# Attention with image prompts on one core: last keys in array halves, context 1 turned by VectorE, prompts in four tiles, inner products moved up, and loads on GpSimd's queue

## The chip, the core and the metric

The kernel runs on one core of a Trainium2 chip. The core has five engines that run side by side, each through its own instructions in order: TensorE (PE in the profile; PEld is its loading of weights, which overlaps with its products), VectorE (DVE), ScalarE (ACT), GpSimd (POOL) and SyncE (SP). They work on SBUF, a memory of 128 partitions, and on PSUM, into which TensorE writes; PSUM has eight banks of 512 float32 per partition. Engines wait for each other by semaphores. Transfers between main memory and SBUF are issued by SP, ACT or POOL and carried out by 16 DMA engines. All data here are float32.

The metric is the time of one execution in microseconds of device time, as the median over several runs. The profile comes from one further execution.

## What is computed

Eight batches (B = 8). Each has 112 queries of 320 channels and a context of 375 rows of 512, of which the last four are image prompts (NIP = 4) and the other 371 are text. There are 20 heads of 16 channels.

```python
q, k_t, v_t = heads(x @ W_q), heads(text @ W_k), heads(text @ W_v)
probs_t = softmax(q @ k_t.T * 16 ** -0.5)             # 112 x 371 for each head
text_out = probs_t @ v_t
k_ip, v_ip = heads(ip @ W_k_ip), heads(ip @ W_v_ip)
qsem = l2norm(probs_t @ text)                         # 112 x 512 for each head
sem = qsem @ l2norm(ip).T                             # 112 x 4
probs_ip = softmax(q @ k_ip.T * 16 ** -0.5 + 0.5 * sem) * spatial_mask
out = (text_out + probs_ip @ v_ip) @ W_out + b_out + x
```

The kernel never forms `probs_t @ text`. Its squared norm is p G p, where p are the unnormalised probabilities and G = text textᵀ, the inner products of the context's rows with each other; G is the same for all heads of a batch. G is symmetric, so only its upper part is made, its diagonal blocks are halved and all of it is doubled.

## The kernel before

**Layout.** Channels lie in three chunks on the partitions: two of 128 and a last one of 64 (`FULL` = 2, `REST` = 64). Heads are worked in five groups of four (`g` = 0 to 4). A head's scores use one of the four 32-row strips of the array (`RG` = 32), so the four heads of a group go side by side. Groups 0 to 3 use the two full chunks; a strip of 32 rows holds two heads there, and a mask on the queries (`emask`, line 353) picks one. Group 4 uses the last chunk. Its 64 channels hold four heads in two strips, so the kernel before spreads them: `spread` (L124) puts 16 columns of zeros behind each head's columns in the last chunk of `W_q` and `W_k`, which makes it 128 wide.

**Keys.** `keys(b)` (L493) makes kT, the channels' chunks by 371 context rows, in three pieces. The first two are full-array products of `wk_sb` with the transposed context `ctxT` (L512). The third is made in two ways. For batches 0 and 7 it is a product like the others with the spread weights (L512 for batch 0, `last_keys`, L526, for batch 7). For batches 1 to 6 `values(b)` (L535) carries 64 extra columns of key weights beside the 320 of `W_v` (L543, 384 wide), POOL spreads the result into `k3` (L552), and three PE transposes (L503) turn it.

**Context.** A context reaches `ctxT` (512 by 384, in four chunks of 128) in one of two ways. For b below `LEAD` = 2, rows are loaded as they are (L156, L158), turned by 12 PE transposes (L414) and copied out of PSUM by ACT and DVE (L422, L424). From batch 2 on, eight transfers (L143, L148) load 32-row blocks of 128 columns and DVE turns them in three stream transposes (L402).

**A group's work.** Scores (L662) on PE; negative row maximum on DVE (L675); exponentials on ACT (L679); a transfer on SP that deals the probabilities into 32-row blocks (`xg`, L686); a stream transpose on DVE (L698, `transposed`); then the big products on PE, probabilities times `u` (L710, `product`), which holds, for each context row, its part of G, a column of ones, the prompts' columns and the values of the group. `placed` (L629) is the POOL copy that puts the next group's values into `u`; it can only run when PE has read the old ones. The product is reduced against p on DVE (L763) and its last 21 columns are copied by ACT (L737). Scores run two groups ahead.

**Next batch's work.** Between groups the function `behind(n)` puts pieces for the next batch on PE: inner products (`gram`, L474, in four column tiles of 32), values, keys, queries (`project_queries`, L319). Its list `turn` says from which pool each piece takes its PSUM bank: `mm` and `sc` have two banks, `qd` has four, which also hold the big products. G goes to `u` through SP (`gram_to_groups`, L488), values through main memory (L561, L573, L582).

**Order.** Every engine's order is the order in which the code is written. The first stage (L1020 to L1064) is written out piece by piece: context 0, its inner products, values and queries of batch 0, first keys, first scores, then context 1's transposes, the second scores, the other keys, and the first of three pieces of batch 1's inner products. `alone(0)` then runs the first group of big products, `behind(0)` puts in the other two pieces of inner products, the prompts' projections (`prompt_projections`, L275; their weights are loaded into `wip` by L1057 and L1058) and one values chunk, and pairs of groups follow. The last batch has its own order from L1314.

**Prompts.** `normalised_prompts` (L247) makes the transposed prompts for all batches at once (32 of them). Their keys and values are two column tiles of 32 rows (L280). `prompt_values` (L589) loads a batch's prompt values, repeated over the 112 partitions, by a transfer on SP; `x_sb`, the queries' input and the residual, is loaded by SP in three parts (L167, L1196, L1236).

Of the kernel before, what the change touches and what calls it, by code (L numbers as in the profile page):

```python
# [20 lines left out]
def kernel(  # L21
# [30 lines left out]
    HN = H * NIP  # L52
    VW = NIP + 1 + D
# [51 lines left out]
    wk_sb = const.tile([P, NE, CP], F32, tag="wk_sb", name="wk_sb")  # L105

    wv_sb = const.tile([P, NE, C + REST], F32, tag="wv_sb", name="wv_sb")
# [16 lines left out]
    def spread(eng, t):  # L124

        v = t[:, :, FULL * P :].rearrange("p k (a r d) -> p k a r d", r=2, d=D)
        for a in (3, 2, 1):
            eng.tensor_copy(v[:, :, a, 0, :], v[:, :, a // 2, a % 2, :])
        eng.memset(v[:, :, :, 1, :], 0.0)


# [3 lines left out]
    def load_ctx(b):  # L135
        ct = io.tile([P, NT, E], F32, tag="ct", name=f"ct_{b}")
        if b >= LEAD:
# [78 lines left out]
    k3 = const.tile([P, NT, GROUP, 2, D], F32, tag="k3", name="k3")  # L216

    def more_constants():
        halves(1)
        nc.gpsimd.memset(k3[:, :, :, 1, :], 0.0)  # L220
        nc.gpsimd.memset(wo_sb[REST:, FULL, :], 0.0)
        for at in attn_ring:
            nc.gpsimd.memset(at[:, C:], 0.0)
# [10 lines left out]
    def order_values():  # L234
# [10 lines left out]
        )  # L245

# [28 lines left out]
    def prompt_projections():  # L275

        ps = bank("ps_kv")
        for e in range(NE):
            for i, w in enumerate((wkip_sb, wvip_sb)):
                nc.tensor.matmul(  # L280
                    ps[i * N : (i + 1) * N, :C],
                    ipT[:, e, :],
                    w[:, e, :],
                    start=(e == 0),
                    stop=(e == NE - 1),
                )
        kv = work.tile([2 * N, C], F32, tag="vip", name="kv", bufs=1)
        nc.scalar.copy(kv, ps[: 2 * N, :C])
        k3p = k3[:N, 0]
        nc.gpsimd.tensor_copy(  # L290
            k3p[:, :, 0, :], kv[:N, FULL * P :].rearrange("n (a d) -> n a d", d=D)
        )
# [3 lines left out]
        for i in range(NC):  # L296
            nc.tensor.transpose(
                ps[:, i * N : (i + 1) * N],
                kv[:N, i * P : (i + 1) * P] if i < FULL else k3p.rearrange("n a r d -> n (a r d)"),
                ident[:N, :N],  # L300
# [11 lines left out]
        nc.sync.dma_start(vipd, kv[N:])  # L312
# [6 lines left out]
    def project_queries(bs):  # L319
# [21 lines left out]
        for i in range(NC):  # L341
# [10 lines left out]
            for r in range(2 if i < FULL else 1):  # L352
# [14 lines left out]
    def begin(b):  # L367
        s = st[b] = dict(ct=loaded.pop(b))
        s["ctxT"] = work.tile([P, NE, TP], F32, tag="ctxT", name=f"ctxT_{b}")
        if b < LEAD:  # L370
            nc.gpsimd.memset(s["ctxT"][:, :, T:], 0.0)

        s["kT"] = work.tile([P, NC, T], F32, tag="kT", name=f"kT_{b}")
        s["k3"] = k3
# [19 lines left out]
    def transposed_context(b):  # L394
# [3 lines left out]
        if b >= LEAD:  # L398
# [94 lines left out]
    def keys(b):  # L493
# [3 lines left out]
        for i in range(NC):  # L497
            ps = bank(f"ps_k_{b}_{i}", spare=0 < b < B - 1 and i == FULL)
            if 0 < b < B - 1 and i == FULL:

                for c in range(NT):
                    rows = min(P, TT - c * P)
                    nc.tensor.transpose(  # L503
                        ps[:, c * P : c * P + rows],
                        s["k3"][:rows, c].rearrange("p a r d -> p (a r d)"),
                        ident[:rows, :rows],
                    )
                nc.scalar.copy(s["kT"][:, i, :TT], ps[:, :TT])
                yield
                return  # L510
# [9 lines left out]
            yield  # L520

    def last_keys(b, ps):

        s = st[b]
        for e in range(NE):
            nc.tensor.matmul(  # L526
                ps[:, :TT],
                wk_sb[:, e, FULL * P :],
                s["ctxT"][:, e, :TT],
                start=(e == 0),  # L530
                stop=(e == NE - 1),
            )
        nc.scalar.copy(s["kT"][:, FULL, :TT], ps[:, :TT])

    def values(b):  # L535
        s = st[b]
        s["vext"] = work.tile([P, NT, C + REST], F32, tag="vext", name=f"vext_{b}", bufs=1)
        ctxT, vext = s["ctxT"], s["vext"]
        w = C + REST if 0 < b < B - 1 else C
        for c in range(NT):  # L540
            ps = bank(f"ps_v_{b}_{c}")
            for e in range(NE):
                nc.tensor.matmul(  # L543
                    ps[:, :w],
                    ctxT[:, e, c * P : (c + 1) * P],
                    wv_sb[:, e, :w],
# [887 lines left out]
```

## Time and profile before

| | |
|---|---|
| median of 3 runs | 419.94 us (419.73 to 420.93) |
| the profiled execution | 421.54 us |
| its span, first to last instruction | 419.8 us |
| granted TensorE clock | 0.999 |
| busy PE, PEld, DVE, ACT, POOL | 411.7, 314.1, 322.2, 185.5, 116.0 us |
| main memory read, written | 19.04 MB, 5.22 MB |

The page of the profile lists busy time by engine, a picture of the span in 40 slices, DMA queues, the chain of work that ended last, and the costliest groups of instructions. The chain is followed back from the last instruction: at each step to what released it, or to the instruction before it on its engine. A group's row reads: line, engine, operation, output from input with partitions by elements, count, then busy time and the mean length of one in ns, then the idle time just before them and what ended it. Instructions on PE overlap, so the mean length of one is longer than the busy time that it adds. A timeline row starts with start and length; a row of stretches has a stretch, its length, and busy times of PE, PEld, DVE, ACT and POOL, the granted clock, the DMA engines' busy share and GB/s. Rows whose engine is written SPq or POOL with `DMA_DIRECT2D` are the issuing of transfers, not the transfers.

### The profile page before, as it was taken

The numbers are of one execution on the slowest core, as the hardware profiler recorded it, in microseconds if no ns is written. First come the engines' busy times: TensorE is split into PE (matmuls) and PEld (weight loads), VectorE is DVE, ScalarE is ACT, GpSimd is POOL, SyncE is SP. The second block draws the span as 40 slices with busy tenths as digits, with TensorE's granted clock in tenths as the row PEclk, the third lists the DMA queues.
The fourth block names the chain that finished last, engine by engine and source line by source line (L and its number), as shares of the span: only waits on it lengthen the run. The fifth ranks groups of instructions, "written<-read, shape, count | busy, mean of one in ns | idle before, by whom it ended". The sixth has DMA issues, their size and how long they took to land.

```text
span 419.8 us, 13826 instructions
## 1 busy us (share of the span) xinstructions
PE 411.7 (98%) x5511; PEld 314.1 (75%) x5511; DVE 322.2 (77%) x684; ACT 185.5 (44%) x634; POOL 116.0 (28%) x278
## 2 busy tenths in 40 slices
PE   8999999999999999999999999999999999999995
PEld 8866686877677786868686877778776888776893
DVE  4054777897887876886888897887788897789964
ACT  3253333334543642514553464333643464246772
POOL 4302310031161352012051225102124126005570
PEclk9999999999999999999999999999999999999999
DMA  8678966778554656577645575575656345575311
GB/s 249 163 190 246 220 157 165 180 187 181 133 156 125 169 127 170 143 162 160 174 116 138 148 173 144 156 186 138 164 150 168 92 118 149 156 177 169 98 34 29
DMA packets 58002, 64.64 MB, mean 154 GB/s; under 512 B 19016, under 2 KB 51760, under 8 KB 57938
## 3 DMA queue, kind: packets, MB, share of 16 engines
q1 hardware_dynamic: 57054, 62.32, 58.5%
q8 instruction: 44, 0.72, 0.7%
q10 hardware_dynamic: 692, 0.89, 0.7%
q0 software_dynamic: 192, 0.55, 0.6%
q14 instruction: 20, 0.16, 0.1%
HBM read 19.04 MB, written 5.22 MB: 58 GB/s over the span
## 4 chain that ended last, share of the span: by engine, by line
PE 87%; DVE 4%; DMA 3%; ACT 2%; SPq 2%; issue 1%; ACTq 0%; POOL 0%; DVEq 0%; POOLq 0%
PE ps_qd L710 39%; PE ps_v L543 15%; PE ps_k L512 10%; PE ps_g L474 8%; PE ps_s L662 5%; PE ps_q L344 3%; PE ps_o L867 2%; DMA xg<-p 1%; DVE xgT L698 1%; PE ps_g L444 1%; DMA vr<-vd 1%; ACT p L679 1%; PE ps_c L414 1%; DVE nmx L675 1%; SPq L488 1%; DMA ct<-in_ctx_dram 1%
## 5 line engine op out<-in xcount | busy, mean ns | idle before, releaser
L710 PE MATMUL ps_qd<-u,xgT 32*112 32x40 f32 (+11 forms) x3840 | 215.7, 351 | 0.4 <-DVE xgT L698 0.4
L710 PEld LDWEIGHTS ps_qd<-u,xgT 32*112 32x112 f32 x3840 | 177.4, 172 | 38.4 <-issue 7.1
L698 DVE STREAM_TRANSPOSE xgT<-xg 128x768 f32<-128x768 f32 (+1 forms) x63 | 123.1, 1976 | 7.1 <-DMA xg<-p 7.1
L679 ACT ACTIVATE p<-ps_s,nmx 112x371 f32<-112x371 f32 x160 | 85.6, 584 | 58.3 <-DVE nmx L675 57.2
L675 DVE TENSOR_REDUCE nmx<-ps_s 112x1 f32<-112x371 f32 x160 | 77.1, 534 | 36.7 <-PE ps_s L662 34.0
L763 DVE CUSTOM_DVE_ANT_0 p<-ps_qd,p 112x371 f32<-112x371 f32 x150 | 72.7, 544 | 15.9 <-ACT pvs L737 10.4
L629 POOL COPY u<-vr 128x64 f32<-128x64 f32 x120 | 26.7, 236 | 185.0 <-PE ps_qd L710 108.0
L543 PE MATMUL ps_v<-wv_sb,ctxT 128*128 128x384 f32 (+1 forms) x192 | 63.8, 479 | 0.3 <-ACT kT L519 0.3
L662 PE MATMUL ps_s<-kT,qm 32*112 32x375 f32 (+1 forms) x320 | 60.8, 486 | 0.0
L543 PEld LDWEIGHTS ps_v<-wv_sb,ctxT 128*128 128x128 f32 x192 | 35.3, 190 | 21.2 <-ACT kT L519 1.2
L512 PE MATMUL ps_k<-ctxT,wk_sb 128*128 128x371 f32 x136 | 45.8, 481 | 0.0
L737 ACT COPY pvs<-ps_qd 112x21 f32<-112x21 f32 x150 | 21.7, 198 | 52.4 <-DVE ss L763 50.1
L512 PEld LDWEIGHTS ps_k<-ctxT,wk_sb 128*128 128x128 f32 x136 | 24.6, 190 | 13.4 <-ACT ctxT L424 0.5
L474 PE MATMUL ps_g<-ctxT 128*32 128x119 f32 (+11 forms) x672 | 33.3, 344 | 0.6 <-POOL ctxT L390 0.6
L474 PEld LDWEIGHTS ps_g<-ctxT 128*32 128x32 f32 x672 | 25.9, 109 | 8.1 <-issue 4.1
L662 PEld LDWEIGHTS ps_s<-kT,qm 32*112 32x112 f32 x320 | 27.1, 171 | 5.0 <-issue 0.5
L550 ACT COPY vext<-ps_v 128x384 f32<-128x384 f32 (+1 forms) x24 | 11.2, 465 | 37.1 <-PE ps_v L543 37.0
L681 ACT COPY ipl<-ps_s 112x4 f32<-112x4 f32 x140 | 24.0, 172 | 0.0
L353 DVE TENSOR_SCALAR qm<-ps_q,emask 128x224 f32<-128x224 f32 (+1 forms) x25 | 9.0, 398 | 18.5 <-PE ps_q L344 18.5
L460 ACT ACTIVATE ug<-ps_g 128x375 f32<-128x375 f32 (+2 forms) x24 | 9.0, 377 | 29.2 <-DMA ct<-in_ctx_dram 8.4
L519 ACT COPY kT<-ps_k 128x371 f32<-128x371 f32 x17 | 8.0, 469 | 30.5 <-PE ps_k L512 30.5
L402 DVE STREAM_TRANSPOSE ctxT<-ct 128x512 f32<-128x512 f32 x18 | 19.3, 1077 | 0.0
(157 smaller groups left out, 311.6 us busy)
## 6 DMA issues: line engine op xcount, KB each, us to landing
xg<-p SPq DMA_DIRECT2D x158, 162.3 KB
u<-ug SPq DMA_DIRECT2D x128, 99.0 KB
ct<-in_ctx_dram SPq DMA_DIRECT2D x24, 176.0 KB
vip<-vipd SPq DMA_DIRECT2D x7, 560.0 KB
vr<-vd SPq DMA_DIRECT2D x20, 120.0 KB
vd<-vext SPq DMA_DIRECT2D x14, 160.0 KB
vd<-vext SPq DMA_DIRECT2D x28, 40.0 KB
ct<-in_ctx_dram SPq DMA_DIRECT2D x4, 256.0 KB
```

The costliest lines, as they stand in the source:

```text
L474: nc.tensor.matmul(ps[p * RG : (p + 1) * RG, s0 : T - t0], ctxT[:, e, t0 + q * RG : t0 + (q + 1) * RG], ctxT[:, e, t0 + s0 : T], start=(e ...
L512: nc.tensor.matmul(ps[:, :TT], wk_sb[:, e, i * P : (i + 1) * P], s["ctxT"][:, e, :TT], start=(e == 0), stop=(e == NE - 1),)
L543: nc.tensor.matmul(ps[:, :w], ctxT[:, e, c * P : (c + 1) * P], wv_sb[:, e, :w], start=(e == 0), stop=(e == NE - 1),)
L629: nc.gpsimd.tensor_copy(region(b, c)[:, :, UV - c * P :], s["vr"][:, c * QN : (c + 1) * QN, g, :])
L662: nc.tensor.matmul(ps[:S, :w], qm[a * RG : (a + 1) * RG, i, r, j * S : (j + 1) * S], s["kT"][a * RG : (a + 1) * RG, i, :w], start=True, st ...
L675: nc.vector.tensor_reduce(nmx, ps[:S, :TT], AX.X, ALU.max, negate=True)
L679: nc.scalar.activation(p, ps[:S, :TT], AF.Exp, bias=nmx)
L681: nc.scalar.copy(s["ipl"][:, groups[g][a], :], ps[:S, TT:T])
L698: nc.vector.transpose(xT[:, j : j + n].rearrange("p j (k q) -> p q j k", q=QN), xg[:, :, j * RG : (j + n) * RG].rearrange("p q (j k) -> p ...
L710: nc.tensor.matmul(banks[a][:S, j * RG : UW], xT[a * RG : (a + 1) * RG, j, :S], region(b, c)[a * RG : (a + 1) * RG, p, q * RG :], start=(j ...
L737: nc.scalar.copy(s["pvs"][:, h, :], ps[:S, TT:UW])
L763: nc.vector.tensor_tensor_reduce(out=p, in0=ps[:S, :TT], in1=p, scale=1.0, scalar=0.0, op0=ALU.mult, op1=ALU.add, accum_out=s["ss"][:, h : ...
```

## The change

1. **Last keys in array halves.** `last_keys` serves all batches. The 64 key columns are no longer spread. Each of the four chunks of E is multiplied twice, into the PSUM partitions 0 to 63 for the first half of the context's rows (`KH` = 186) and into 64 to 127 for the second half. ACT copies each half twice, so that kT's last chunk holds the 64 channels two times, on partitions 0 to 63 and 64 to 127. `W_q`'s last 64 columns are likewise there twice, by one POOL copy. Group 4 then works as the others do: `scores` takes strips 0, 2, 1, 3 for its four heads, with the mask; so queries need both masks in the last chunk too (`range(2)`, one more DVE operation for each projection). Gone are `spread`, `k3` with its copies and transposes, and the 64 extra columns of the values.
2. **Context 1 by VectorE.** Context 1 is loaded and turned as batches 2 to 7 are, and its place is earlier: right after batch 0's inner products in the code.
3. **Prompts in four tiles.** Keys and values of the prompts are four column tiles of 32 rows and 160 columns; three ACT copies and one POOL copy take them out, and two transfers instead of one write the values to main memory.
4. **Inner products moved up.** All three pieces of batch 1's inner products stand in the first stage, before the first big products; `behind(0)` has none.
5. **GpSimd's queue.** `prompt_values` and the second and third part of `x_sb` are issued by POOL instead of SP.

The lists of banks (`turn`) are changed accordingly.

```diff
-            if 0 < b < B - 1 and i == FULL:
-                for c in range(NT):
-                    rows = min(P, TT - c * P)
-                    nc.tensor.transpose(
-                        ps[:, c * P : c * P + rows],
-                        s["k3"][:rows, c].rearrange("p a r d -> p (a r d)"),
-                        ident[:rows, :rows],
-                    )
...
+        last_keys(b, bank(f"ps_k_{b}_{FULL}", spare=0 < b < B - 1))
+        yield
...
     def last_keys(b, ps):
         s = st[b]
         for e in range(NE):
...
+            for n in range(2):
+                nc.tensor.matmul(
+                    ps[n * REST : (n + 1) * REST, : min((n + 1) * KH, TT) - n * KH],
+                    wk_sb[:, e, FULL * P :],
+                    s["ctxT"][:, e, n * KH : min((n + 1) * KH, TT)],
+                    start=(e == 0),
+                    stop=(e == NE - 1),
+                )
+        for n in range(2):
+            t = slice(n * KH, min((n + 1) * KH, TT))
+            for m in range(2):
+                nc.scalar.copy(
+                    s["kT"][m * REST : (m + 1) * REST, FULL, t],
+                    ps[n * REST : (n + 1) * REST, : t.stop - t.start],
+                )
...
-        w = C + REST if 0 < b < B - 1 else C
...
-                    wv_sb[:, e, :w],
+                    wv_sb[:, e, :],
...
+        rg = a
+        if i == FULL:
+            rg, r = a // 2 + 2 * (a % 2), a % 2
...
-        if b >= LEAD:
+        if b > 0:
...
             for i, w in enumerate((wkip_sb, wvip_sb)):
...
+                for n, part in enumerate(parts):
+                    m = 2 * i + n
+                    nc.tensor.matmul(
+                        ps[m * N : (m + 1) * N, : C // 2],
+                        ipT[:, e, :],
+                        w[:, e, part],
...
-        nc.sync.dma_start(
+        nc.gpsimd.dma_start(
             st[b]["vip"].rearrange("p n h d -> p (n h d)"),
...
     drain(products)
+    drain(transposed_context(1))
     gram_to_groups(0, range(QN - 1))
...
-    spread(nc.gpsimd, wq_sb)
-    nc.gpsimd.tensor_copy(wv_sb[:, :, C:], wk_sb[:, :, FULL * P : C])
-    spread(nc.gpsimd, wk_sb)
+    nc.gpsimd.tensor_copy(wq_sb[:, :, C:], wq_sb[:, :, FULL * P : C])
...
-    turn[:] = ["mm", "qd", "qd"]
-    drain(transposed_context(1))
-    prompts_behind(1)
...
-    run(("g", 1), lambda: gram(1))
+    turn[:] = ["mm", "mm", "sc"]
+    run(("g", 1), lambda: gram(1), NT)
...
-                turn[:] = ["sc", "mm", "qd", "mm"]
-                nc.sync.dma_start(x_sb[:, 1:5, :], x[1:5].rearrange("b s c -> s b c"))
+                turn[:] = ["qd", "mm"]
+                nc.gpsimd.dma_start(x_sb[:, 1:5, :], x[1:5].rearrange("b s c -> s b c"))
...
-            gr(nb, 2)
             if n:
+                gr(nb, 2)
                 f(b - 1)
...
-                nc.sync.dma_start(x_sb[:, 5:, :], x[5:].rearrange("b s c -> s b c"))
+                nc.gpsimd.dma_start(x_sb[:, 5:, :], x[5:].rearrange("b s c -> s b c"))
```

83 lines of the change are left out of this document (27 added, 56 removed).

## The prediction

> **What bounds the kernel now.** I read the page from the top, then the chain, then the groups by shape.
>
> ```profile
> span 419.8 us, 13826 instructions
> ...
> PE 411.7 (98%) x5511; PEld 314.1 (75%) x5511; DVE 322.2 (77%) x684; ACT 185.5 (44%) x634; POOL 116.0 (28%) x278
> ...
> PE 87%; DVE 4%; DMA 3%; ACT 2%; SPq 2%; issue 1%; ACTq 0%; POOL 0%; DVEq 0%; POOLq 0%
> ```
>
> PE is busy for 98% of the span and carries 87% of the chain; the next engine, DVE, has 77%. So a microsecond of PE work removed is a microsecond of time, unless PE then waits for something. Two stretches say where DVE could take over (columns: stretch, length, then busy time of PE, PEld, DVE, ACT, POOL, each with its count):
>
> ```profile
> 109.00:158.00 49.00, 49.00 (x763) 37.23 (x762) 40.81 (x91) 23.41 (x86) 17.85 (x31) 1.00 0.55 141
> ...
> 378.00:392.00 14.00, 14.00 (x221) 10.32 (x220) 13.39 (x27) 9.68 (x33) 8.06 (x15) 1.00 0.52 149
> ```
>
> In mid-kernel DVE has 8.2 us free in 49, ACT half of it, POOL most of it. In the ending (378 to 392) DVE is nearly as full as PE, and a gain on PE alone is worth little there.
>
> The chain in order of time gives the price of each PE piece (start, length, piece, instructions):
>
> ```profile
> 13.69 2.16 PE ps_v L543 x8
> ...
> 25.22 0.85 PE ps_q L344 x6
> 26.07 1.43 PE ps_c L414 x12
> 27.50 1.21 PE ps_s L662 x6
> 28.70 5.18 PE ps_k L512 x16
> 33.89 2.64 PE ps_g L474 x27
> 36.53 1.15 PE ps_qd L710 x10
> ...
> 41.88 2.19 PE ps_g L474 x43
> 44.07 2.21 PE ps_kv L280 x16
> 46.28 2.78 PE ps_v L543 x8
> 49.05 1.15 PE ps_qd L710 x10
> ...
> 101.51 0.32 PE ps_k L503 x3
> 101.83 2.51 PE ps_k L512 x8
> 104.34 5.16 PE ps_v L543 x16
> ...
> 138.09 0.47 PE ps_k L503 x3
> 138.56 4.64 PE ps_g L474 x71
> 143.19 2.78 PE ps_v L543 x8
> ```
>
> Three prices follow. Each matrix product in the code is issued as two instructions (eight for four chunks of E). Batch 0's values, 320 columns wide, take 2.16/8/320 = 0.844 ns per column and instruction; the later ones, 384 wide, 2.58 (5.16/2), which is 0.42 more. Second, column tiles stream side by side: the prompts' 16 instructions of 320 columns in two tiles take 2.21, as long as 8 of them would (2.16). Third, a change of tile shape costs 0.15 to 0.20: the three key transposes take 0.47 between inner products and other shapes and 0.32 among full-array work, and the first values after another shape 2.78 against 2.58.
>
> **The change, part by part, in PE time.**
>
> *Keys' last 64 channels.* They come from two half-array tiles of 186 columns: 16 instructions, 8 side by side, 8 x 186 x 0.844 = 1.26. No row has 64-column tiles; the nearest are the 32-column tiles above, so 1.26 is the low end, and the high end is the two halves one after the other, 2.51. I take 1.26, because the prompts' row shows two tiles at the price of one. With a shape change in (0.15) and, where full-array work follows, one out (0.20):
> - batch 0: 2.59 (half of 5.18) becomes 1.41, -1.18.
> - batches 2, 4, 6 (inner products follow): the transposes' 0.47 become 1.41, +0.94; three value chunks lose 3 x 0.42 = 1.26. Net -0.32 each.
> - batches 1, 3, 5 (full-array work on both sides): 0.32 becomes 1.61, +1.29, against -1.26: nothing. Here the change only pays for itself.
> - batch 7: 2.59 becomes 1.41, -1.18 on PE, in the ending.
>
> The Trainium skill (TensorEngine Tiling (Array Packing), Key Properties) says that changing the tiling mode, not just the tile, drains TensorE. The trace agrees on the sign with the 0.15 and 0.20 above; were the drains free, batches 1, 3 and 5 would gain 0.32 each and the sum would be about 1 us better.
>
> *Context 1 by DVE.* PE loses 1.43 (12 transposes), DVE gets three stream transposes of 1.077 for one copy, ACT loses two copies:
>
> ```profile
> L402 DVE STREAM_TRANSPOSE ctxT<-ct 128x512 f32<-128x512 f32 x18 | 19.3, 1077 | 0.0
> L353 DVE TENSOR_SCALAR qm<-ps_q,emask 128x224 f32<-128x224 f32 x15 | 6.1, 444 | 4.0 <-PE ps_q L344 4.0
> ...
> L508 ACT COPY kT<-ps_k 128x371 f32<-128x371 f32 x6 | 3.0, 507 | 1.1 <-PE ps_k L503 1.1
> ...
> L339 ACT COPY xT<-ps_x 64x224 f32<-64x224 f32 x3 | 1.1, 352 | 0.0
> ```
>
> The transposes stand in DVE's hole of 11.40 us ahead of the first masked queries, so they cost nothing if the context has landed. The danger is the queue behind them. POOL's copy of batch 1's prompts waits for the last transpose, and behind it, on POOL, now stand the zeroing of xT and the copy of wq_sb, which ran from 14.56; PE needs the zeros by about 20.4:
>
> ```profile
> 14.56 0.28 POOL L327 MEMSET xT<- 64x224 f32 x1
> ...
> 20.30 0.82 PE L344 MATMUL ps_q<-xT,wq_sb 128*128 128x112 f32 x6
> ...
> 21.16 0.58 DVE L353 TENSOR_SCALAR qm<-ps_q,emask 128x112 f32<-128x112 f32 x2 [11.40 <-PE ps_q L344]
> ```
>
> When does the context land? Now the loads are over by about 13.2 (15 packets in 13.2 to 14.5). It comes in rows of 512 B instead of 2 KB: four transfers of 352 rows and four of 19. Where such rows fill the queue they take 3 x 16 x 1.211/1219 = 47.7 ns each:
>
> ```profile
> DMA packets 15, 0.02 MB, mean 13 GB/s; under 512 B 7, under 2 KB 7, under 8 KB 15
> ```
> ```profile
> q1 hardware_dynamic: 1219, 0.61, 121.1%
> ```
>
> Over 16 engines 1408 rows take 4.2, some 2 more than now, so about 15; the 76 odd rows add 0.2 if spread and 3.6 if they all go through one engine. So the last rows land between 15.2 and 19. Two transposes need only the big transfers and end at 17.2; the third ends between 18.3 and 20.1, and POOL's copy and zeros (0.28 each at most) between 18.8 and 20.7. Against 20.4 that is a wait of 0 to 0.3; I take 0.2, and up to 1 for the range, because transfers of this stage may also meet others.
>
> *Inner products moved up.* No PE work changes, but the order does. These rows (the packets are those of 42.0 to 42.7) set the order's cost:
>
> ```profile
> 32.74 3.12 DVE L698 STREAM_TRANSPOSE xgT<-xg 128x768 f32<-128x768 f32 x2 [2.51 <-DMA xg<-p]
> ...
> 37.03 0.50 SPq L122 DMA_DIRECT2D wip<-in_L_xattn_W_v_ip_dram  x1
> ```
> ```profile
> DMA packets 105, 0.15 MB, mean 210 GB/s; under 512 B 6, under 2 KB 105, under 8 KB 105
> ```
> ```profile
> 43.97 4.50 DVE L698 STREAM_TRANSPOSE xgT<-xg 128x1536 f32<-128x1536 f32 x2
> ```
> ```profile
> L698 DVE STREAM_TRANSPOSE xgT<-xg 128x1536 f32<-128x1536 f32 x17 | 51.5, 3027 | 0.0
> ```
>
> Chain of the first stage: queries end at 26.07, scores 1.21, keys 2.59 and 1.41, whole inner products 4.64 (row at 138.56): 35.92. The first transposed probabilities, which hang on the first scores and not on what changes here, are there at 35.86, so the first big products start at 35.9 instead of 36.53 and end at 41.3 instead of 41.88. The cover is thus used to the end: any lateness of the probabilities now shows at once. Next come the prompts. Their 16 instructions become 32 of 160 columns in four tiles, 8 x 160 x 0.844 = 1.08, -1.1. But their weights are asked for at 37.03 now, at the end of a run of issues on SP that starts from the first scores and does not change. The packets between 42.0 and 42.7 are all under 2 KB, so the weights' 5 KB packets have started by then, and I let them land by 42.7. The prompts' bank is now one of the four that the big products hold; DVE frees the first when the first of its four sums is done, and it begins them when the products end, so before 42.7 too.
>
> So PE stands idle from 41.3 to 42.7, does the prompts until 43.8 and a values chunk (2.78 - 0.42) until 46.2. DVE, whose group transposes started at 43.97 behind the sums of the first products, starts 0.6 earlier, and its first transposition (3.0) ends at 46.4. The second group starts at 46.4 instead of 49.05: **-2.65** of a PE saving of 1.43 + 1.18 + 1.1 + 0.42 = 4.13. The weights' late landing, hidden today under 2.19 of inner products, takes most of the rest.
>
> *After that:* batch 1's two other value chunks -0.84 and its keys +1.29: +0.45; batches 2, 4, 6: -0.96; 3 and 5: 0.06. Together **-0.45**. Ending: -1.18 on PE beside a full DVE, and the bank is held longer by four ACT copies; I take **-0.3**, ends 0 and -1.2.
>
> *Cover.* ACT's four copies of 64 x 186 stand for one of 507: by the 352 row at most 4 x 0.35 = 1.4, +0.9 per batch, some 7 in all, on an engine 56% idle; a bank comes free 0.9 later, under inner products of 4.64 or keys of 2.51. DVE gets a second masking of the last queries, four of 0.444 and a shorter one, within its 8.2 free per 49. The spreading and key copies on POOL go.
>
> *POOL's queue.* POOL issues two loads of x and seven prompt-value transfers in SP's place:
>
> ```profile
> L118 POOL DMA_DIRECT2D wo_sb<-in_L_xattn_W_out_dram x1 | 0.9, 921 | 0.0
> ...
> L1219 POOL DMA_DIRECT2D bias_sb<-in_L_xattn_b_out_dram x1 | 0.5, 543 | 0.0
> ...
> L629 POOL COPY u<-vr 128x64 f32<-128x64 f32 x120 | 26.7, 236 | 185.0 <-PE ps_qd L710 108.0 <-DMA u<-ug 30.0 <-DMA vr<-vd 24.0
> ```
>
> 112 rows cost 0.543, 256 cost 0.921, so 2.6 ns a row more: seven of 0.54, and about 1.4 and 1.1 for the 448 and 336 rows of x, 6.3 in all. Behind them stand the placements (L629) that PE needs; these waited 108 us for PE itself, so I take 0, with 6.3 as the far end. On SP nine issues go and four come (context 1 in eight transfers, not four); I count nothing for either.
>
> **Sum.** 0.2 - 2.65 - 0.45 - 0.3 = -3.2. The profiled execution took 421.54, with a span of 419.8; less 3.2 that is 418.3 and 416.6. The median of the runs is 419.94, 1.6 below the profiled one, which gives 416.7.
>
> **Rivals.**
> - *The gain passes whole* (weights and banks early enough, ending follows PE): 4.13 + 0.45 + 1.18 = -5.8, 414.2. For it: PE carries the chain. Against: the landing at 42.
> - *The halves do not run side by side.* Then batches 0 to 6 cost 1.25 more each, 8.75, and batch 7's 0.3 is lost: 425.7, slower than before. It decides from 3.2/56 = 57 ns per step: above 214 instead of 157. Against it: the prompts' row; for it: two tiles of 64 need double the weights per step.
> - *POOL becomes the queue PE waits for*, by its transfers or the zeros behind the context: up to 6.3, 423; it decides when half of that shows.
> - *Shape changes dearer* for 64-column tiles, 0.5 (the longest wait before big products that the profile puts down to issue, below) instead of 0.15 (eight times) and 0.20 (three times): +3.7, 420.4, no change.
>
> ```profile
> PEld ps_qd L710 <- issue: 7.1, 16, 0.5
> ```
>
> **How the numbers follow.** Measurement tells 0.3%, 1.3 us, from no change: faster below 418.7, slower above 421.2. Chances: forecast 0.62 (own range 415.2 to 418.6), whole gain 0.14, shape changes 0.08, halves 0.07, POOL 0.09. So faster 0.76, same 0.08, slower 0.16. The range from 414.0 to 421.0 leaves out the slower cases and a little below.
>
> **What would show it.** In the new profile: 16 key instructions at about 1.3 to 1.4 in the chain; values at 2.16; prompts at 1.1 after a PE gap of about 1.4 near 41 to 43; second group of big products near 46.4; PE before the first queries waiting 0.2 or less on POOL; 378 reached about 3.1 earlier. The forecast is wrong if the halves take 2.5, if L629 delays PE, or if the context lands after 20.

## The result, and the profile after

The changed kernel takes 433.52 us (median of four runs, 428.47 to 434.83), the kernel before 420.44 in the same session. The ratio is 1.0279, with a 95% interval of 1.0223 to 1.0334: slower by 2.8%, where 416.7 us and a gain of 0.8% were forecast. Some executions of a kernel are slower as a whole, at a lower granted clock; the ratios, here and below, leave these out, while the medians take them in.

The page of the profile after (the queue lines are packets, MB and share of 16 engines):

```profile
span 431.8 us, 14046 instructions
...
PE 418.2 (97%) x5609; PEld 329.4 (76%) x5609; DVE 325.4 (75%) x691; ACT 190.3 (44%) x658; POOL 117.2 (27%) x272
...
q1 hardware_dynamic: 56128, 57.29, 54.0%
q0 software_dynamic: 1328, 5.57, 5.2%
...
PE 87%; DMA 4%; DVE 3%; ACT 2%; issue 1%; SPq 1%; POOL 1%; ACTq 0%; DVEq 0%; POOLq 0%
```

PE's busy time has gone up by 6.5 us though the change takes work from it (e17 below, with the same 5609 instructions, is busy for 408.6); part of that is work at half clock, shown in the last section. POOL's queue (q0) now carries 5.57 MB. The chain in order of time (start, length, piece) shows where the time went:

```profile
37.98 6.61 DMA wip<-in_L_xattn_W_v_ip_dram
44.63 2.35 PE ps_kv L274 x28
46.98 2.86 PE ps_v L531 x8
49.84 1.15 PE ps_qd L695 x10
...
91.86 2.94 PE ps_qd L695 x66
94.80 0.70 issue
95.51 4.40 PE ps_qd L695 x48
...
103.78 1.41 PE ps_k L509 x15
...
107.87 4.31 PE ps_v L531 x16
...
151.09 2.93 PE ps_qd L695 x62
154.02 1.29 issue
155.31 6.08 PE ps_qd L695 x48
```

The prices of PE work are those forecast: last keys 1.41, values 4.31 for sixteen. What is new are waits. The prompts' product starts at 44.63, when its weights land; it then takes 2.35 instead of 1.1, at half clock (at the full clock, in e3 below, the same 28 of its 32 instructions take 1.28). And in the middle of the big products PE stops (the pieces named issue), first at 94.80, longest at 154.02. Around the second stop, with the half clock behind it, 4.9 us are lost: the lag behind the kernel before is 2.85 us at 148.82 and 7.75 where the next keys start. Of these 0.55 are not the stop's, since e1 below has no stop there and loses as much (e12 tells why).

The starts of the big products tell how much each stretch costs. The table gives, for some kernels of this study, the start of a group in us and in brackets its distance from the kernel before:

| kernel | batch 0, 2nd | batch 1, 1st | batch 1, 3rd | batch 2, 4th | batch 6, 4th | batch 7, 5th |
|---|---|---|---|---|---|---|
| before | 48.98 | 89.41 | 109.43 | 166.41 | 361.54 | 403.27 |
| after | 49.77 (+0.8) | 89.71 (+0.3) | 112.11 (+2.7) | 173.31 (+6.9) | 372.73 (+11.2) | 417.06 (+13.8) |
| e1, values on SP | 46.89 (-2.1) | 88.54 (-0.9) | 111.73 (+2.3) | 168.58 (+2.2) | 365.19 (+3.7) | 407.33 (+4.1) |
| e3, both on SP | 48.04 (-0.9) | 88.97 (-0.4) | 113.52 (+4.1) | 170.38 (+4.0) | 368.27 (+6.7) | 410.32 (+7.1) |
| e4, before, both on POOL | 48.54 (-0.4) | 88.97 (-0.4) | 108.99 (-0.4) | 168.29 (+1.9) | 366.23 (+4.7) | 409.60 (+6.3) |
| e9, e3 with loads put off | 47.80 (-1.2) | 87.74 (-1.7) | 108.18 (-1.3) | 166.40 (0.0) | 363.43 (+1.9) | 406.04 (+2.8) |
| e12, e3 with rows mended | 47.31 (-1.7) | 87.59 (-1.8) | 111.07 (+1.6) | 167.34 (+0.9) | 362.74 (+1.2) | 404.79 (+1.5) |
| e13, all of it | 49.42 (+0.4) | 89.07 (-0.3) | 109.50 (+0.1) | 165.78 (-0.6) | 361.51 (0.0) | 404.05 (+0.8) |
| e17, weights by ACT | 49.14 (+0.2) | 88.79 (-0.6) | 109.22 (-0.2) | 165.50 (-0.9) | 360.72 (-0.8) | 402.93 (-0.3) |

Each row is one execution. That of e3 took 427.17 us, 3.0 above the median of its kernel; that of e4 426.53, 2.3 below. The first stage scatters most: e2, e3, e5, e6 and e8 below are the same program up to 70 us, and their second group started at 50.92, 48.04, 47.88, 46.95 and 50.86. A difference of 2 us in the first column is therefore no effect of an edit by itself. The table stops at the start of the last group, since the spans mislead: the traced execution of the kernel before takes 4.6 us from the end of its last computation (415.24) to that of its span, and e10, below, 3.1 (from 417.96).

### The profile page after: what moved, and what is told of

It is laid out like the page before. It is cut to its first block, busy times and chain, and to the rows that moved or that the text cites. A ratio compares the mean times of both kernels' runs of the same rounds, so it can differ in the third digit from the quotient of the medians.

```text
span 431.8 us, 14046 instructions
## 1 busy us (share of the span) xinstructions
PE 418.2 (97%) x5609; PEld 329.4 (76%) x5609; DVE 325.4 (75%) x691; ACT 190.3 (44%) x658; POOL 117.2 (27%) x272
## 3 DMA queue, kind: packets, MB, share of 16 engines
q0 software_dynamic: 1328, 5.57, 5.2%
## 4 chain that ended last, share of the span: by engine, by line
PE 87%; DMA 4%; DVE 3%; ACT 2%; issue 1%; SPq 1%; POOL 1%; ACTq 0%; DVEq 0%; POOLq 0%
PE ps_qd L695 42%; PE ps_v L531 13%; PE ps_k L492 9%; PE ps_g L466 6%; PE ps_s L647 5%; PE ps_q L337 3%; DMA xg<-p 2%; PE ps_k L509 2%; PE ps_o L852 2%; DMA wip<-in_L_xattn_W_v_ip_dram 2%; PE ps_g L436 1%; DVE xgT L683 1%; ACT p L664 1%; PE ps_w L423 1%; DVE nmx L660 1%
## 5 line engine op out<-in xcount | busy, mean ns | idle before, releaser
L695 PE MATMUL ps_qd<-u,xgT 32*112 32x40 f32 (+11 forms) x3840 | 224.4, 355 | 6.2 <-ACT kT L519 2.1
L695 PEld LDWEIGHTS ps_qd<-u,xgT 32*112 32x112 f32 x3840 | 187.7, 173 | 41.4 <-issue 8.1
L683 DVE STREAM_TRANSPOSE xgT<-xg 128x768 f32<-128x768 f32 (+1 forms) x63 | 123.5, 1976 | 27.8 <-DMA xg<-p 24.6
L647 PE MATMUL ps_s<-kT,qm 32*112 32x375 f32 (+1 forms) x320 | 64.3, 485 | 0.0
L531 PE MATMUL ps_v<-wv_sb,ctxT 128*128 128x320 f32 x192 | 56.6, 441 | 0.3 <-ACT kT L499 0.3
L492 PE MATMUL ps_k<-ctxT,wk_sb 128*128 128x371 f32 x128 | 43.6, 484 | 0.0
L647 PEld LDWEIGHTS ps_s<-kT,qm 32*112 32x112 f32 x320 | 30.5, 171 | 4.7 <-ACT p L664 0.4
L492 PEld LDWEIGHTS ps_k<-ctxT,wk_sb 128*128 128x128 f32 x128 | 23.0, 190 | 13.2 <-issue 1.3
L394 DVE STREAM_TRANSPOSE ctxT<-ct 128x512 f32<-128x512 f32 x21 | 22.4, 1077 | 5.3 <-DMA ct<-in_ctx_dram 5.3
L538 ACT COPY vext<-ps_v 128x320 f32<-128x320 f32 x24 | 10.2, 425 | 30.6 <-PE ps_v L531 30.6
L346 DVE TENSOR_SCALAR qm<-ps_q,emask 128x224 f32<-128x224 f32 (+1 forms) x30 | 10.6, 398 | 10.3 <-PE ps_q L337 10.3
```

Source lines behind the costliest of these rows:

```text
L394: nc.vector.transpose(ctxT[:, :, c * P : (c + 1) * P].rearrange("p e (j i) -> p j e i", i=RG), ct[:, some, :].rearrange("p j (k e) -> p j ...
L492: nc.tensor.matmul(ps[:, :TT], wk_sb[:, e, i * P : (i + 1) * P], s["ctxT"][:, e, :TT], start=(e == 0), stop=(e == NE - 1),)
L531: nc.tensor.matmul(ps[:, :C], ctxT[:, e, c * P : (c + 1) * P], wv_sb[:, e, :], start=(e == 0), stop=(e == NE - 1),)
L647: nc.tensor.matmul(ps[:S, :w], qm[rg * RG : (rg + 1) * RG, i, r, j * S : (j + 1) * S], s["kT"][rg * RG : (rg + 1) * RG, i, :w], start=True ...
L683: nc.vector.transpose(xT[:, j : j + n].rearrange("p j (k q) -> p q j k", q=QN), xg[:, :, j * RG : (j + n) * RG].rearrange("p q (j k) -> p ...
L695: nc.tensor.matmul(banks[a][:S, j * RG : UW], xT[a * RG : (a + 1) * RG, j, :S], region(b, c)[a * RG : (a + 1) * RG, p, q * RG :], start=(j ...
```

## Experiments: the queue

Theory A: a transfer on another queue stands beside those of SP and takes their share of the DMA engines. Theory B: the queue is innocent. Theory C: POOL's time for issuing is the cost.

**e1, e2, e3: one or both kinds of transfer back on SP.**

```diff
     def prompt_values(b):
-        nc.gpsimd.dma_start(          # e1, e3
+        nc.sync.dma_start(
...
-                nc.gpsimd.dma_start(x_sb[:, 1:5, :], ...)   # e2, e3; x[5:] as well
+                nc.sync.dma_start(x_sb[:, 1:5, :], ...)
```

> The changed kernel with the seven prompts' values issued by SP again; the inputs x stay on POOL's queue. Theory A (two queues share the DMA engines: a transfer on POOL's queue no longer stands behind the xg transfers in one line but beside them, and makes them land late): the losses of the pairs behind a prompt-value transfer go, 4.9 us at 151 to 164, 2.1 at 254 to 264, 2.1 at 353 to 364 and 2.6 at the end, so 421 to 424 us. Theory B (the queue is innocent, the prologue's gap and lateness carry on): stays at 432 to 434. Theory C (POOL's own time for issuing holds up its copies into u): seven issues of 0.6 us, so 429 to 430.

> The changed kernel with the two transfers of x issued by SP again; the prompts' values stay on POOL's queue. Theory A: the transfers from SP at 62 to 71 no longer take 6 to 7 us to land, SP is not behind at 70 to 92, and the loss of 2.0 us at 92 to 102 goes; the losses behind the prompts' values stay: 430 to 432 us. Theory B: 433. Theory C: two issues of 0.9 us, about 432.

> The changed kernel with x and the prompts' values all on SP again: what is left of the change is the last keys in halves, the context by DVE, the prompts in four tiles and the inner products moved up. Theory A: 417 to 420 us, near or below the kernel before, and no stretch at half clock behind 150. Theory B: 430 to 434. Theory C: about 427.

**e4: the kernel before with the queue's part alone** (the same lines the other way).

> The kernel before with only the queue changed: x and the prompts' values issued by POOL. Theory A: loses like the changed kernel behind 90, 428 to 434 us. Theory B: 420 to 421. Theory C: at most 6 us more, 424 to 426.

Measured: e1 424.13 us (ratio to before 1.0066, 1.0038 to 1.0093), e2 432.77 (1.0203, 1.0141 to 1.0265), e3 424.15 (1.0062, 1.0031 to 1.0092), e4 428.87 (1.0181, 1.0118 to 1.0244). The prompts' values on POOL's queue cost 9.4 us (433.52 to 424.13), x next to nothing (e1 and e3 are equal), and on the kernel before both cost 7. That is theory A's size, and above what C allowed for e4. But e3 does not reach the 417 to 420 that A also gave: the rest of the change loses too.

The stretch around 150 us shows the mechanism. In the timeline of SP after, four xg transfers are issued:

```profile
139.75 3.53 SPq L671 DMA_DIRECT2D xg<-p  x4
```

In that of POOL, the prompts' values are issued in the middle of them:

```profile
141.60 0.59 POOL L574 DMA_DIRECT2D vip<-vipd  x1
```

The view of the tile vip gives their landing:

```profile
DMA to landing us min/median/max: 8.8/8.8/8.8
```

And in the timeline of DVE the last xg are awaited:

```profile
151.35 1.57 DVE L683 STREAM_TRANSPOSE xgT<-xg 128x768 f32<-128x768 f32 x1 [4.32 <-DMA xg<-p]
```

In e1's timeline of DVE the same transposition has no wait,

```profile
146.56 1.60 DVE L683 STREAM_TRANSPOSE xgT<-xg 128x768 f32<-128x768 f32 x1
```

and its timeline of SP has the 560 KB behind the four xg:

```profile
139.37 3.53 SPq L671 DMA_DIRECT2D xg<-p  x4
142.95 0.54 SPq L574 DMA_DIRECT2D vip<-vipd  x1
```

So on SP the line kept them behind. On POOL's queue they start when POOL comes to them, and the last xg are there only 8.1 us after SP has issued them (139.75 + 3.53 to 151.35); in e1 they are there 3.7 us after, at the latest (142.90 to 146.56). Over the whole run DVE waits 24.6 us for xg (total, times, longest):

```profile
DVE xgT L683 <- DMA xg<-p: 24.6, 10, 4.3
```

and in the kernel before 7.1:

```profile
DVE xgT L698 <- DMA xg<-p: 7.1, 6, 2.5
```

The Trainium skill (DMA: Bandwidth & Descriptors, Issuing engines are not separate DMA queues) says that transfers of any issuing engine run on the same 16 DMA engines "and interleave with each other, regardless of the engine that started them". The rows above agree: POOL's 560 KB were under way from 141.60 to 150.4, and SP's last xg were awaited until 151.35.

**e5, e6: whose queue, and how many bytes.** e5 is e3 with the prompts' values issued by ACT. e6 is e3 with a quarter of each on POOL:

```diff
-        nc.sync.dma_start(st[b]["vip"]..., vipd[...])
+        for eng, n0, n1 in ((nc.gpsimd, 0, 1), (nc.sync, 1, NIP)):
+            eng.dma_start(st[b]["vip"][:, n0:n1]..., vipd[b * NIP + n0 : b * NIP + n1, :]...)
```

> As with both on SP (424.15 us), but the prompts' values are issued by ACT, so in a third line that costs POOL nothing. Theory A (the transfer stands beside the xg transfers instead of behind them, and takes their share of the DMA engines): slower again by 4 to 9 us, 428 to 433, with xg landing 5 to 8 us after its issue where it took 3. Theory C (POOL's time for issuing is what costs): 424, with perhaps 1 us for ACT's own seven issues.

> As with both on SP (424.15 us), but a quarter of each prompt-value transfer (140 of 560 KB) is issued by POOL and three quarters by SP. Theory A: the loss goes with the bytes that POOL's queue carries, a quarter of 9 us, so 425 to 427. Theory C: the loss goes with the number of issues, which is the seven of the changed kernel, so 432 to 434.

Measured: e5 434.83 (1.0304, 1.0253 to 1.0355), e6 429.32 (1.0197, 1.0163 to 1.0231). e5 excludes theory C: without any work for POOL the loss is whole. It also excludes that the kind of POOL's queue is to blame (software_dynamic on the page), since ACT's transfers go through a queue of the same kind as SP's. e6 fits neither: a quarter of the bytes brings 5.2 of 9.4 us. So the bytes alone do not set the price. How it divides between them and the mere presence of a second line stays open. No run has POOL issue the values only after the last xg, which would tell the line from the moment of the issue (141.60 on POOL, 142.95 on SP in e1).

## Experiments: what else was lost

With both queues as before, the change still runs 0.6% above the kernel before. First thought: the prologue's gain is real but SP, which issues without a break from 55 to 92 us, gives it back (S), or the moved prologue does harm (P).

**e7: halves and prompts in four tiles alone,** the prologue as before. **e8: e3 with eight of SP's issues (the second batch's values and the prompts') made by ACT.**

```diff
-            values_to_dram(nb, nc.sync)
+            values_to_dram(nb, nc.scalar if b == 0 else nc.sync)
...
-            nc.sync.dma_start(vipd[:, part], kv[...])
+            nc.scalar.dma_start(vipd[:, part], kv[...])
```

> The kernel before with the last keys in halves and the prompts in four tiles alone: context 1 by PE, the inner products and both queues as before. Theory S (the prologue's gain on PE is real but is given back by 92 us, because SP issues without a break from 55 to 92 and the xg of the second pair lands when it lands): within 1.5 us of both on SP, 422 to 424.5. Theory P (the moved prologue itself does harm): 1 to 2 us below the kernel before, 419.5 to 421.

> As with both on SP (424.15 us), but the second batch's values (six issues) and the prompts' two are written out by ACT, so that SP has eight issues of 0.4 to 0.6 us less between 70 and 76 us. Theory S: the xg at 76 are issued 3 us earlier, the second pair no longer waits for them, and 2 to 3 us of the prologue's gain stay: 421 to 422. Theory P, or a bound by the DMA engines' bytes rather than by SP's issuing: 424, as before.

Measured: e7 425.78 (1.0105, 1.0063 to 1.0146), e8 424.22 (1.0056, 1.0030 to 1.0083). Both theories fall. The halves alone lose as much as e3 (the intervals overlap), so the moved prologue is not needed for the loss; and fewer issues on SP help nothing. In e7 as in e3 the loss sits in one place, between the first and the third group of batch 1 (e3 in the table: -0.4 to +4.1).

There the kernels that are early wait, and those that are late do not. In e1, whose second group started at 46.89, DVE's transposition ahead of the second group of batch 1 starts late:

```profile
92.11 1.57 DVE L683 STREAM_TRANSPOSE xgT<-xg 128x768 f32<-128x768 f32 x1 [4.72 <-DMA ct<-in_ctx_dram]
```

In e8, whose second group started at 50.86, it hardly waits:

```profile
90.79 1.62 DVE L683 STREAM_TRANSPOSE xgT<-xg 128x768 f32<-128x768 f32 x1 [0.42 <-DMA xg<-p]
```

Either way the third group of batch 1 starts at about the same time, 111.73 and 112.01. So something other than PE seems to set that time, and the next runs seek it among the transfers.

**e9, e10, e11: loads put off** (theory T: the bytes that are moved between 42 and 92 us set the time). e9 is on e3, e10 on the kernel before, e11 on e7.

```diff
-                nc.sync.dma_start(x_sb[:, 1:5, :], x[1:5]...)
-                load_channels(nc.gpsimd, wo_sb, w_out)
+                nc.sync.dma_start(x_sb[:, 1:3, :], x[1:3]...)
...
-                nc.sync.dma_start(x_sb[:, 5:, :], x[5:]...)      # behind the third group of batch 0
...
+            if b == 1:                                           # behind(n), group 1
+                load_channels(nc.gpsimd, wo_sb, w_out)
+            if b == 1:                                           # behind(n), group 3
+                nc.sync.dma_start(x_sb[:, 3:, :], x[3:]...)
```

> The halves, the context by DVE, the prompts in four tiles and the inner products moved up, with both queues as before (424.15 us when it ran so), and 1.2 MB of transfers taken out of the stretch from 42 to 80 us: of x only the second and third batch are loaded at 43 (287 KB for 573), the other five (717 KB) at about 115 us, in place of 430 KB at 75; the output weights (328 KB), first used at 128 us, at about 112 in place of 47. Theory T (the stretch from 42 to 92 is bound by its transfers, so the prologue's gain on PE is given back in a wait for xg at 88 to 97 and its half clock): the wait at 88 to 97 goes, and the gain stays: 416 to 419 us. Theory P (PE's own order or the shape changes cost it): 423 to 425, as without this.

> The kernel before with the same transfers put off, and nothing else of the change. Theory T: its prologue on PE is 2 us later than that of the changed kernel, so the transfers hold it up only in part of the runs: 419 to 421. Theory P: 421 to 422, as without this.

> The halves and the prompts in four tiles alone (425.78 us when they ran so), with the same transfers put off. Theory T: their loss was the wait at 88 to 97 and goes: 418.5 to 421, between the two other kernels of this call. Theory P: 424 to 426.

Measured: e9 422.86 (1.0036, 1.0006 to 1.0066), e10 422.32 (1.0021, 1.0003 to 1.0039), e11 423.86 (1.0052, 1.0028 to 1.0075). All three miss theory T's times, yet at the place it spoke of T is right. A stretch of 6 us in e3 (columns as in the prediction; the last two are the DMA engines' share and GB/s):

```profile
52.00:58.00 6.00, 6.00 (x129) 5.74 (x123) 4.43 (x11) 1.83 (x8) 0.71 (x3) 1.00 1.01 186
```

and in e9:

```profile
52.00:58.00 6.00, 6.00 (x130) 5.80 (x124) 4.58 (x13) 2.12 (x8) 0.81 (x4) 1.00 0.66 169
```

The second transposition of the pair behind it, in e3's timeline of DVE:

```profile
92.20 1.58 DVE L683 STREAM_TRANSPOSE xgT<-xg 128x768 f32<-128x768 f32 x1 [4.55 <-DMA ct<-in_ctx_dram]
```

and in e9's:

```profile
87.63 1.60 DVE L683 STREAM_TRANSPOSE xgT<-xg 128x768 f32<-128x768 f32 x1 [1.00 <-DMA xg<-p]
```

In e9 the DMA engines are no longer full from 52 on, the wait is 1.00 instead of 4.55 (its end is put down to the context's transfer in e3 and e1, to xg in e7, where it is 4.83), and e9 keeps its lead through the third group of batch 1 (-1.3, where e3 has +4.1). Then it loses 1.5 by the second group of batch 2 (0.5 of it is the longer key piece that every kernel with halves has there; for most of the rest the late x stood on SP ahead of values that POOL places), and 1.6 more by the fourth group of batch 6. In e10 the second group started at 51.53: the prompts' weights landed at 46.44, where the trace of the kernel before has them at 42.68. Fewer bytes are asked for in e10 up to there, not more, so scatter between executions is the likelier cause. Chain of e10:

```profile
37.80 8.64 DMA wip<-in_L_xattn_W_v_ip_dram
46.48 2.34 PE ps_kv L280 x14
...
51.60 1.15 PE ps_qd L710 x10
```

Two questions were left: what the kernels with halves lose from batch 2 on, and the weights.

**e12: the row groups of the last scores** (theory R). The change keeps head a of the last tile on row group 0, 2, 1, 3; its products use row group a. e12 is e3 with the tile's 64 channels in head order 0, 2, 1, 3 in queries, keys and prompts' keys:

```diff
         rg = a
         if i == FULL:
-            rg, r = a // 2 + 2 * (a % 2), a % 2
+            r = a // 2
```

> As with both on SP (424.15 us), but the last tile's four heads are kept in the order 0, 2, 1, 3, so that each head's scores use the row group that its products use (0, 1, 2, 3 instead of 0, 2, 1, 3). Theory R (scores of heads 0 and 1 on row groups 0 and 2 collide with the products of heads 2 and 3): the groups that lead these scores, the third of batches 2, 4 and 6, take 0.5 us less, their four starts come in pairs again, and the whole is 1 to 2 us faster, 422 to 423. Theory N (the row group does not matter, what is lost is DVE's lateness): 424.

Measured: 422.37 us (1.0032, 1.0004 to 1.0060). The interval overlaps e3's, so the trace decides. The timeline of PE (start, length, line, instructions) in the third group of batch 2, up to the next keys, in the kernel before:

```profile
155.03 0.57 PE L662 MATMUL ps_s<-kT,qm 32*112 32x375 f32 x2
...
155.43 0.48 PE L662 MATMUL ps_s<-kT,qm 32*112 32x375 f32 x2
...
156.60 0.58 PE L512 MATMUL ps_k<-ctxT,wk_sb 128*128 128x371 f32 x1
```

in e11 (halves, rows as changed):

```profile
155.67 0.56 PE L647 MATMUL ps_s<-kT,qm 32*112 32x375 f32 x1
...
156.03 0.52 PE L647 MATMUL ps_s<-kT,qm 32*112 32x375 f32 x2
...
156.35 0.47 PE L647 MATMUL ps_s<-kT,qm 32*112 32x375 f32 x1
...
157.61 0.58 PE L492 MATMUL ps_k<-ctxT,wk_sb 128*128 128x371 f32 x1
```

and in e12:

```profile
156.80 0.59 PE L658 MATMUL ps_s<-kT,qm 32*112 32x375 f32 x2
...
157.20 0.50 PE L658 MATMUL ps_s<-kT,qm 32*112 32x375 f32 x2
...
158.39 0.89 PE L501 MATMUL ps_k<-ctxT,wk_sb 128*128 128x371 f32 x2
```

Before, two scores (two instructions each) start together, beside products on the other two row groups. In e11 they start one after the other, the first and the last instruction alone, and by the code one of the two is on a row group that products hold. From the third group's start to the next keys it took 5.05 us before (151.55 to 156.60), 5.61 in e11 (from 152.00), 5.12 in e12 (from 153.27). From the third group's start to the fourth's, e12 gains 0.79 on the kernel before, e11 only 0.29; e3, e7 and e9 gain 0.30, 0.30 and 0.31, and e13 and e17, which have the rows of e12, 0.79 each. Theory R is shown; it gives 0.5 us in batches 2, 4 and 6.

**e13, e14: all of it, and the same without halves.** The prompts' weights go ahead of the second group's xg, and the loads to places where the DMA engines were idle. e14 keeps the keys of the kernel before.

```diff
     gram_to_groups(0, (QN - 1,))
+    load_embed(nc.sync, wkip_sb, w_k_ip)
+    load_embed(nc.sync, wvip_sb, w_v_ip)
...
             values_to_dram(nb, nc.sync, 0, 2)
+            if b == 1:
+                load_channels(nc.sync, wo_sb, w_out)
+                nc.sync.dma_start(x_sb[:, 3:5, :], x[3:5]...)
+            if b == 3:
+                nc.sync.dma_start(x_sb[:, 5:, :], x[5:]...)
```

> As the run before, and the prompts' weights issued by SP ahead of the second group's xg, x loaded in three parts (43, 111 and 210 us) and the output weights at 111 us, where the DMA engines were idle. Theory T with theory R: weights landed by 41 us, second group at 46 to 47 us, no wait at 88 to 97, no half clock: 418 to 420 us, below the kernel before. If only the scores counted: 422 to 423.

> The kernel before, its keys by transposes as they were, with the context by DVE, the inner products moved up, the weights earlier and the transfers put off as in the run before. Theory T: the prologue's 2 us stay and nothing is lost behind: 418.5 to 420 us. Theory P (the moved prologue is worth nothing): 421 to 422.

Measured: e13 419.74 (0.9980, 0.9958 to 1.0003), e14 420.19 (0.9967, 0.9942 to 0.9992). The wait at 88 to 97 is gone in both, and at the fourth group of batch 4 e13 is 1.3 us ahead of the kernel before. But the second group starts at 49.42, not 46 to 47. Now the xg are late. Chain of e13:

```profile
37.22 9.07 DMA xg<-p
46.37 2.91 DVE xgT L694
49.42 1.22 PE ps_qd L706 x10
```

**e15 to e18: the weights at 15 us,** ahead of batch 0's inner products on their way to the groups, by SP (e15 on e13, e16 on e14) or by ACT (e17, e18).

```diff
+    load_embed(nc.sync, wkip_sb, w_k_ip)        # nc.scalar in e17, e18
+    load_embed(nc.sync, wvip_sb, w_v_ip)
     gram_to_groups(0, range(QN - 1))
```

> As the run with everything (419.74 us), but the prompts' weights issued at 15 us, ahead of the first groups of inner products. If the transfers bound the prologue (theory T): second group at 46.5 to 47 us in place of 49.4, the rest as there, so 417 to 418 us. If another wait takes their place, at the first group above all (its inner products land later): 419 to 420.

> As the run without the halves (420.19 us), but the prompts' weights issued at 15 us. Theory T: second group at 46.5 to 47 us in place of 49.5: 417.5 to 418.5 us. Otherwise 420.

> As the run with everything (419.74 us), but the prompts' weights issued at 15 us by ACT. If SP's stand was the cause of the last loss: first group at 36.5 to 37 us, second at 46.5 to 47, 417 to 418 us. If the transfers' bytes are (the weights take 4 us of all engines wherever they stand): first group at 38 or later, 420 to 422.

> As the run without the halves (420.19 us), but the prompts' weights issued at 15 us by ACT. If SP's stand was the cause: second group at 46.5 to 47 us, 417.5 to 418.5. Otherwise 420 to 422.

Measured: e15 422.70 (1.0027, 1.0002 to 1.0052), e16 423.75 (1.0066, 1.0040 to 1.0092), e17 419.37 (0.9950, 0.9931 to 0.9968), e18 421.22 (1.0005, 0.9988 to 1.0021). In e15 SP itself stood still until the weights were there (waits of SP: total, times, longest):

```profile
SPq L489 <- DMA wip<-in_L_xattn_W_v_ip_dram: 3.2, 1, 3.2
```

and the first group started at 39.52, the second at 51.52. By ACT the first started at 38.53 and the second at 49.14, between the two theories. SP still waits for the weights in e17, though ACT issues them:

```profile
SPq L489 <- DMA wip<-in_L_xattn_W_k_ip_dram: 2.5, 1, 2.5
```

The inner products that SP issues there do not use the weights; why it waits for them is not shown. How much of the first group's lateness is this wait, and how much the 1.3 MB themselves, was not separated.

e17 has the lowest time of the study: 0.5% below the kernel before, and 3.2% below the changed one (0.9950/1.0279). What the halves themselves are worth, once the rows are mended, is small: e17 is faster than e18, which lacks them and the prompts in four tiles (their intervals lie apart), but e13 and e14, and e15 and e16, cannot be told apart. The page of e17:

```profile
span 418.0 us, 14045 instructions
...
PE 408.6 (98%) x5609; PEld 324.0 (78%) x5609; DVE 326.9 (78%) x691; ACT 190.0 (45%) x658; POOL 112.1 (27%) x269
```

## Why the prediction was wrong, point by point

The forecast was 16.8 us too low (433.52 against 416.7). Two of its steps failed. One took the move to POOL's queue as free; it makes 9.4 of the 16.8 (the changed kernel against e1). The other took the stretch behind the second group as PE's alone; with the start of that group it makes most of the rest. In e1's trace 4.4 us are lost between the second group of batch 0 and the third of batch 1 (-2.1 to +2.3), and 1.5 by the scores' row groups. The kernel before was itself 2.0 us higher in e1's session (421.9) than the 419.94 that the forecast started from.

**POOL's queue, taken as 0: the step that failed.** It cost 9.4 us, above the far end of 6.3 and beyond the rival's 423. The rival named the right queue and the wrong price: it was built from POOL's issue time and from who stands behind on POOL. The sentence "On SP nine issues go and four come", for which nothing was counted, should have asked what the nine had been *behind*. On SP they stood behind xg by order alone; moved, they lost it, and the engine that waited was DVE, for SP's own transfers.

**Price of the halves, 1.41 and 1.61: right.** The chain has 1.40 to 1.41, and keys after them 2.69 for 2.51, so 1.59. Values came to 2.15 against 2.16. So the rivals of serial halves and of dearer shape changes are refuted. The prompts in four tiles were priced too low, 1.08: at the full clock their 32 instructions took 1.50 in e12 (no shape change was counted for them). But the step that summed only keys and values (-0.32 in batches 2, 4, 6) left out the diff's line on `rg`: the scores' row groups cost 0.5 in each of these. That was in the diff, and no row of the prediction bears on it.

**Second group at 46.4 (-2.65): missed in the changed kernel (49.77), nearly reached in e1 (46.89) and e6 (46.95).** The order of PE's work was right, the wait mis-sized: "I let them land by 42.7" holds for the kernel before (42.68), but in the runs the weights landed at 42.9 (e1), 43.97 (e9), 44.4 (e3), 44.6 (after), 45.8 (e8), 46.4 (e10), and in the changed kernel and in e8 the prompts then ran at half clock. One landing time was taken for a fixed one. Also the first group was forecast at 35.9; it started at 36.3 (e1) to 37.4 (e3). There the inner products' own transfer, POOL's placements and the zeroing that POOL does behind them end last (in the profile after at 34.69, 35.47 and 36.68, against 36.79 for the group).

**"After that -0.45": the prices were right, the path was not.** The stretch to 112 was taken as PE's, but transfers end it, and what PE gains ahead is given back as a wait. In the kernel before this was close: DVE waited 0.64 us until 88.97, in e3 4.55 until 92.20. e9 shows that the loads of x and of the output weights, put off, take the wait away. What makes it in e7, whose prologue is the old one, was not settled.

**Ending -0.3: 0.1 to 0.9 the other way.** From the first to the last group of batch 7 the kernels without halves took 25.0 to 25.1 us; those with halves whose queue was as before took 25.2 (e7 and e11) to 26.0 (e9). PE's gain on the last keys came, and the four copies of ACT, counted as covered by other work, have no cover there. Chain of e11, where the second pair of scores starts at 387.94, 0.94 behind the kernel before:

```profile
386.92 0.31 ACT kT L519
387.24 0.31 ACT kT L519
387.56 0.32 ACT kT L519
387.93 0.57 PE ps_qd L695
```

**Context 1 by VectorE** did what was forecast for it: no wait of the first queries on POOL stands in the chain.

## What to carry to other kernels

A transfer moved to another queue does not only save its issue: here it lost its place behind the transfers that had to go first. So list what it stood behind, and who waits for those. And where a chain is nearly all TensorE, as here, a gain in one stage passes on only if the transfers of the next had slack; the wait rows of the engine that consumes them show beforehand whether they had any (DVE's 0.64 us in the kernel before said that they had none).

## What the runs showed of the hardware that was not expected

Short stops of PE can cost a second time. Two stretches of the profile after at half clock (the column behind the five engines is the granted clock):

```profile
44.60:48.00 3.40, 3.37 (x30) 2.19 (x31) 2.69 (x1) 0.85 (x3) 0.33 (x3) 0.50 1.07 218
...
157.20:160.60 3.40, 3.40 (x33) 2.55 (x30) 2.64 (x12) 0.71 (x4) 2.23 (x2) 0.50 0.67 193
```

and the stretch ahead of the second:

```profile
153.80:157.20 3.40, 2.11 (x30) 1.42 (x27) 3.37 (x7) 2.46 (x9) 0.20 (x1) 1.00 0.13 32
```

After 3.4 us in which PE was busy for 2.11, with one stop of 1.29, the clock was halved for 3.4 us, which costs some 1.7 (an estimate: half of 3.4). In e3 a stop of 0.97 was followed by such a stretch; in e1 one of 1.50 was not, and in e2 one of 2.20. What tells them apart is not shown. The Trainium skill (TensorE: Matmul & The Clock Gate, What's actually happening) gives a window of 3413 ns, the length seen here, but has the clock fall after an idle window of that length; here it fell after one in which PE was busy for more than half, so the measurement differs.

SP's line also stopped where no data called for it: in e15 its next issue waited 3.2 us for the weights, which it does not use, and in e17, where ACT had issued the weights, 2.5.
